# Attention without a partner pass: four heads at once, and the output list cut into halves of the queries

## The chip, the cores and the metric

The kernel runs on one core of one Trainium2 chip. The metric is the device time of one execution in microseconds, as the median of several runs. Engines are named as in the profile: PE is TensorE (matmuls; PEld its weight loads), DVE is VectorE, ACT is ScalarE, POOL is GpSimd, and SP is the queue from which the DMAs of this kernel are issued. A profile comes from one profiled execution. "Granted clock" is the share of TensorE's full clock that the throttle let through.

## What is computed

Six sublayers act on an input of 8 sequences, 1024 tokens and 256 features, all in float32: a mixture of experts, causal attention, the same mixture of experts again, then a channel mix, a state-space layer and the channel mix again. The change touches only the attention, and the front of the second mixture of experts, which is run from the attention's work lists. Cut to these:

```python
def _L0_attn_ref(x, w_qkv, w_out, b_out):        # x: 8 x 1024 x 256, 16 heads of 16
    qkv = jnp.einsum('btd,de->bte', x, w_qkv).reshape(B, T, 3, h, Hd)
    ...
    logits = jnp.einsum('bhqd,bhkd->bhqk', q, k) * scale
    logits = logits + (1.0 - mask)[None, None, :, :] * big_neg      # causal
    attn = jax.nn.softmax(logits, axis=-1)
    out = jnp.einsum('bhqk,bhkd->bhqd', attn, v)
    ...
    return jnp.einsum('btd,de->bte', out, w_out) + b_out

x = x + 0.5 * _L0_ffn_ref(_layernorm(x), ...)
x = x + _L0_attn_ref(_layernorm(x), L0_attn_w_qkv, L0_attn_w_out, L0_attn_b_out)
x = x + 0.5 * _L0_ffn_ref(_layernorm(x), ...)     # its front: logits = xf @ Wr + br, softmax
...
```

## The kernel before

**Passes and units.** The 16 heads of a sequence are worked on in 4 groups of 4 heads (`HG`), so there are 32 groups. Group t needs two things in turn: the maximum of each query's logits (queries on the partitions, `self.rows`), and then, with the maximum folded into the transposed queries, the exponentials (keys on the partitions, `self.cols`) and their products with the values. `Attention.run` pipelines the two: in pass t it takes the maxima of group t (`now`) and, beside them, the exponentials of group t - 1 (`old`). Passes are numbered from 0 to 32. Pass 0 has no `old` and pass 32 has no `now`: these are the two passes without a partner. Each pass has 12 units (u = 0 to 11); a unit is one tile of 128 rows with 128 to 512 columns for each of the 4 heads. The widths of units 0 to 11 in `old` are 512, 384, 256, 128, then five times 512, then 384, 256, 128; in `now` they are 512, 384, 256, 128, four times 512, and 512, 384, 256, 128.

**Inside a unit.** A unit is written in two parts. Part 0 issues the logits (L724) of heads 0 and 1 for `now` and of heads 2 and 3 for `old`; part 1 has them the other way round. A head fills 32 rows of the array, so the four heads of a part lie in different row groups and can run side by side. The results go to PSUM: `s1`, 3 banks, for `now`, and `s2`, 3 banks, for `old`. VectorE takes the maxima from s1 (L737, L740), ScalarE the exponentials from s2 into `pT` (L767), GpSimd cuts the diagonal block (L773). The products with the values (`sums`, L787) of a unit follow in part 0 some units later (`LAG`), collect in one bank `po`, and are copied to `so` (L793) and stored to the DRAM tensor `kept` (L796) once for each half of 512 queries: at the end of unit 3's columns for queries 0 to 511, and at the end of unit 11's for 512 to 1023. `less_max` (L749 to L758) sends the negated maxima through DRAM into rows of the transposed queries, in unit 4 of a pass for the first half and in unit 0 of the next for the second.

**Work lists.** Everything else is cut into steps and dealt out between the units by `Lists`. A list is a generator that yields `""` (a step that has no matmul) or `"pe"` (one that has). In each part one `""` step is taken, and in part 1 of each unit but 0 and 4 also one `"pe"` step; the first list whose next step is of the wanted kind gives it. `drain` runs all remaining steps of a list at once. The lists are:

- `steps_in`: layer norm, transposes, queries and keys (pq, L692), values (pv, L655) of the next sequence; added in front in unit 2 of a sequence's third pass, drained at the end of the fourth. `steps_qk` (four pq) is the second half of queries and keys; added in front in unit 2 of a sequence's first pass.
- `steps_out`: division by the sum of the exponentials and projection. It loads the sums from `kept` (over_p, L809) and the unnormalised output (oT, L811), takes the reciprocal (L816), sends it through DRAM (over_d, L819; over, L821), spreads it over the partitions with a matmul (pr, L828) and multiplies oT by it (L833), four times; then four projections (pp, L841), each added to `xt` (L847). There are eleven `""` steps ahead of the first pr. At its end it goes on with `store` and `steps_front`, the front of the second mixture of experts: layer norm, four transposes (tr, L673, copied by ScalarE, L871), four router matmuls (pl, L880; bias added by VectorE, L884), softmax (L890 to L900) and a store.

All matmuls of the lists share one PSUM bank (`mm`). `bank` first flushes the `Pipe`, which issues what reads the bank before, so the next matmul of a list waits for that reader. The list `outs` of sequence b is added in unit 3 of the first pass in which `old` belongs to sequence b + 1 (pass 4b + 5), has four passes, and is drained where the next one is added. The one of the last sequence runs alone after the loop. Each engine works through its instructions in the order in which they are issued.

Of the kernel before, what the change touches and what calls it, by code (L numbers as in the profile page):

```python
# [8 lines left out]
F32 = mybir.dt.float32  # L9
# [3 lines left out]
ALU = mybir.AluOpType  # L13
# [4 lines left out]
P = 128  # L18
D = 256
KC = D // P  # L20
# [10 lines left out]
H = 16  # L31
HD = 16
HS = 32
HG = P // HS
NG = H // HG
# [461 lines left out]
class Attention:  # L497
# [5 lines left out]
    W = 512  # L503
# [211 lines left out]
                to, self.padded[name, p % 2][i].rearrange("h s t -> (h s) t")  # L715
            )

    def logits(self, name, out_of, heads):

        got = {}  # L720
        for h in heads:
            lhsT, rhs = out_of(slice(h * HS, (h + 1) * HS))
            s = self.pools[name].tile([P, self.W], F32, name=name)
            self.net.nc.tensor.matmul(s[:, 0 : rhs.shape[-1]], lhsT, rhs, start=True, stop=True)  # L724
            got[h] = s
        return got
# [70 lines left out]
                q.kept[g * HG : (g + 1) * HG, :, a : a + W].rearrange("h s t -> (h s) t"), so  # L797
            )

    def steps_out(self, q, store):  # L800


        net, nc = self.net, self.net.nc
        T, W = net.T, self.W
        yield ""
        n = H // KC
        q.oT = self.pools["oT"].tile([P, KC, T], F32, name="oT")
        sp = self.pools["over"].tile([P, H * T // P], F32, name="over_p")
        nc.sync.dma_start(sp, q.kept[:, HD, :].rearrange("h (i t) -> h i t", t=H * T // P))  # L809
        for k in range(KC):  # L810
            nc.sync.dma_start(q.oT[:, k, :], q.kept[k * n : (k + 1) * n, 0:HD, :])  # L811
        for _ in range(3):
            yield ""

        yield ""
        nc.vector.reciprocal(sp, sp)  # L816
        yield ""
        d = self.pools["dram"].tile([H, T], F32, name="over_d")
        nc.sync.dma_start(d.rearrange("h (i t) -> (h i) t", t=H * T // P), sp)  # L819
        q.over = self.pools["over"].tile([H, T], F32, name="over")  # L820
        nc.sync.dma_start(q.over, d)  # L821
        for _ in range(5):
            yield ""
        for t0 in range(0, T, W):
            for k in range(KC):
                yield "pe"
                pr = self.bank([P, W], "pr")
                nc.tensor.matmul(  # L828
                    pr, self.spread[:, k, :], q.over[:, t0 : t0 + W], start=True, stop=True
                )  # L830

                def take(o=q.oT[:, k, t0 : t0 + W], pr=pr):
                    nc.vector.tensor_tensor(o, pr, o, ALU.mult)  # L833

                self.pipe.filled(take)
        for c0 in range(0, net.NT, 2):
            yield "pe"
            po = self.bank([P, 2, D], "pp")
            for c in range(2):
                for k in range(KC):  # L840
                    nc.tensor.matmul(  # L841
                        po[:, c, :], q.oT[:, k, (c0 + c) * P : (c0 + c + 1) * P],
                        self.wo[:, k, :], start=(k == 0), stop=(k == KC - 1),
                    )

            def take(x=q.x[:, c0 : c0 + 2, :], po=po):
                nc.vector.tensor_tensor(x, x, po, ALU.add)  # L847

            self.pipe.filled(take)
        yield ""  # L850
        self.pipe.flush()
        yield from store(q.x, q.b)

    def steps_front(self, moe, x, b, rows, S):
# [61 lines left out]
    class Lists:  # L916
# [28 lines left out]
    def run(self, pools, load, store):  # L945
        net = self.net
        self.pools, self.pipe, work = pools, self.Pipe(), self.Lists()
        net.nc.scalar.preload_act_table_set("natural_log_exp_and_others")
        seqs = [self.Sequence(b) for b in range(net.B)]
        groups = [(q, g) for q in seqs for g in range(NG)]  # L950
        LAG, U = 2, len(self.rows)
        ins = work.add(self.steps_in(seqs[0], lambda x: load(x, 0)))
        work.drain(ins)
        behind = []
        outs = ins

        for t in range(len(groups) + 1):
            now = groups[t] if t < len(groups) else None
            old = groups[t - 1] if t else None
            if now:  # L960
                q, g = now
                nxt = seqs[q.b + 1] if q.b + 1 < net.B else None
                qT, kT = self.q[t % 3], self.k[t % 3]
            if old:
                oqT, okT = self.q[(t - 1) % 3], self.k[(t - 1) % 3]
            for u in range(U):
                if now:
                    i, k0, k1 = self.rows[u]
                if old:
                    a, j = self.cols[u]  # L970
                    q0 = max(a, j * P)
                    pT = pools["pT"].tile([P, HG, self.W], F32, name="pT")
                for part, (ha, hb) in enumerate((((0, 1), (2, 3)), ((2, 3), (0, 1)))):
                    if now:
                        sa = self.logits(
                            "s1", lambda r: (qT[r, i * P : (i + 1) * P], kT[r, k0:k1]), ha
                        )
                    if old:
                        sb = self.logits(
                            "s2", lambda r: (okT[r, j * P : (j + 1) * P], oqT[r, q0 : a + self.W]),  # L980
                            hb,
                        )
                    self.pipe.flush()
                    if now:
                        self.maxima(self.rows[u], t, sa)
                    if old:
                        self.weights(self.cols[u], sb, pT)
                    if part == 0:
                        while len(behind) > LAG - bool(old):
                            self.sums(*behind.pop(0))  # L990
                        work.take("")
                        continue
                    if old:
                        self.causal(self.cols[u], pT)
                        behind.append((self.cols[u], *old, pT))
                    if u == 0 and old:
                        self.less_max(t - 1, 1)
                    elif u == 4 and now:
                        self.less_max(t, 0)
                    else:  # L1000
                        work.take("pe")
                    work.take("")
                if u == 2 and now:
                    if g == 1:
                        work.drain(qk)
                    if g < NG - 1:
# [30 lines left out]
class Layer1:  # L1037
# [9 lines left out]
    W = 512  # L1047
# [855 lines left out]
```

## Time and profile before

| what | us |
|---|---|
| median of 3 runs | 5663.02 (5660.18 to 5664.28) |
| the profiled execution | 5670.78 |
| its span, first to last instruction | 5668.9 |
| mean granted clock of TensorE | 0.890 |

The median is of the plain runs; the profile's numbers belong to the one profiled execution, whose span is 0.1% above that median. Within it, from the trace's windows:

| stretch, us from the span's start | what runs | length | PE busy | DVE busy | ACT busy | clock |
|---|---|---|---|---|---|---|
| 705.4 to 754.1 | pass 0 (`now` alone) | 48.7 | 44.7 | 26.9 | 2.6 | 0.72 |
| 754.1 to 2169.7 | passes 1 to 31 | 1415.6 | 1398.6 | 961.0 | 827.2 | 0.99 |
| 2169.7 to 2230.8 | pass 32 (`old` alone) | 61.1 | 55.0 | 0.9 | 23.4 | 0.56 |
| 2230.8 to 2268.6 | out list of the last sequence | 37.8 | 17.9 | 6.5 | 1.3 | 0.62 |
| 2268.6 to 2294.6 | its front of the mixture of experts | 26.0 | 12.0 | 10.5 | 4.3 | 0.58 |

A pass with both partners lasts 1415.6 / 31 = 45.7 us. The rest of the span, before and behind, belongs to stages that the diff doesn't touch. In the lines of the profile that follow, a timeline row has the start, the length, the engine, the source line, the operation, the tile written and the tiles read, the number of equal records merged, and in brackets the idle time before it with what ended it; a float32 matmul leaves two records for each matmul issued. A row of the windows has the stretch, its length, each engine's busy time with its number of records, then the granted clock, the share of the DMA engines and GB/s. Ends of matmuls are modelled, so a busy PE isn't one at its peak.

### The profile page before, as it was taken

To read this page: it belongs to the slowest core of one execution; us is meant where nothing else is said; L and a number is where in the kernel's file an instruction comes from. 1 tells how busy PE (TensorE), PEld (TensorE's weight loads), DVE (VectorE), ACT (ScalarE), POOL (GpSimd) and SP (SyncE) were. 2 spreads that over 40 slices of the span, in tenths; PEclk is the share of its full clock that TensorE was granted. 3 is DMA by queue.
4 is the path that set the end of the run, shared out by engine and by line. 5 is a ranking of instruction groups with operands and counts; after the bars stand their busy time and mean duration, and the time that the engine had idled before them with its cause. 6 is when DMAs were issued, how large, how long until landed. Compare 5 with 4: busy or idle time off the path is not lost.

```text
span 5668.9 us, 60303 instructions
## 1 busy us (share of the span) xinstructions
PE 4660.3 (82%) x21302; PEld 2227.0 (39%) x21302; DVE 3431.4 (61%) x5653; ACT 2505.6 (44%) x4152; POOL 2205.0 (39%) x1801
## 2 busy tenths in 40 slices
PE   5599699999999998399776778788787778878867
PEld 5355434444444443255532233333333324333324
DVE  4532166667666762633107877777767777677884
ACT  2011145666565553011144645465464645546443
POOL 1244201111111110234316656556555666556662
PEclk7699889999999997599887889889898888989888
DMA  6123312122221220223206454535536463454652
GB/s 201 33 57 60 79 37 75 58 74 68 81 74 59 77 69 27 68 49 62 44 13 156 134 145 122 153 98 143 138 105 158 110 163 108 112 153 114 169 137 63
DMA packets 252976, 545.28 MB, mean 96 GB/s; under 512 B 29681, under 2 KB 143681, under 8 KB 252674
## 3 DMA queue, kind: packets, MB, share of 16 engines
q1 hardware_dynamic: 228098, 507.34, 32.1%
q0 software_dynamic: 24576, 34.10, 3.7%
q8 instruction: 168, 2.75, 0.2%
q14 instruction: 134, 1.10, 0.1%
HBM read 400.31 MB, written 141.03 MB: 95 GB/s over the span
## 4 chain that ended last, share of the span: by engine, by line
PE 25%; DVE 13%; ACT 6%; issue 5%; DMA 2%; POOL 1%; SPq 0%; DVEq 0%; POOLq 0%; ACTq 0%
DVE h L1719 8%; PE y L1647 5%; PE pc L1366 4%; PE pr L1261 4%; PE pk L1239 4%; PE pu L1417 2%; DVE hc L1724 2%; PE pp L1501 2%; ACT h L1625 2%; PE pd L1432 1%; ACT xn L1195 1%; PE px L1396 1%; DMA sdu<-du 1%; DVE ln_st L1182 1%; ACT L1131 1%
## 5 line engine op out<-in xcount | busy, mean ns | idle before, releaser
L767 ACT ACTIVATE pT<-s 128x512 f32<-128x512 f32 (+3 forms) x1536 | 670.7, 488 | 554.9 <-PE s L724 546.7
L1625 ACT ACTIVATE h<-sdl,A 128x1024 f32<-128x1024 f32 x512 | 567.0, 1112 | 644.4 <-DVE hc L1724 622.4
L724 PE MATMUL s<-kT,qT 32*128 32x512 f32 (+3 forms) x3072 | 839.5, 540 | 12.9 <-DVE mx L740 8.0
L1647 PE MATMUL y<-hc,pick 128*32 128x512 f32 x2048 | 648.5, 714 | 227.6 <-DVE hc L1724 227.6
L724 PE MATMUL s<-qT,kT 32*128 32x512 f32 (+3 forms) x3072 | 763.7, 547 | 13.3 <-ACT pT L767 13.3
L1616 POOL TENSOR_TENSOR dbu<-sdu,b 128x1024 f32<-128x1024 f32 x256 | 602.3, 2353 | 405.3 <-DMA sdu<-du 217.5
L1719 DVE TENSOR_TENSOR_SCAN h<-h,dbu 128x1024 f32<-128x1024 f32 x256 | 586.1, 2289 | 184.4 <-ACT h L1625 159.8
L1719 DVE TENSOR_TENSOR_SCAN h<-h,sdu 128x1024 f32<-128x1024 f32 x256 | 586.2, 2290 | 160.6 <-ACT h L1625 146.3
L1724 DVE TENSOR_TENSOR hc<-h,c 128x1024 f32<-128x1024 f32 x512 | 625.6, 1222 | 30.4 <-PE y L1647 2.5
L773 POOL TENSOR_SCALAR_AFFINE_SELECT pT<-pT 128x512 f32<-128x512 f32 x256 | 162.4, 634 | 1180.7 <-ACT pT L767 1097.2
L1616 POOL TENSOR_TENSOR sdu<-sdu,b 128x1024 f32<-128x1024 f32 x256 | 602.4, 2353 | 14.4 <-DMA b<-bc 3.7
L724 PEld LDWEIGHTS s<-kT,qT 32*128 32x128 f32 x3072 | 327.6, 187 | 437.1 <-DVE mx L740 184.6
L466 ACT ACTIVATE mid<-pm,bu 128x512 f32<-128x512 f32 x192 | 131.6, 686 | 734.3 <-PE pm L462 734.3
L737 DVE TENSOR_REDUCE part<-s 128x1 f32<-128x512 f32 x512 | 329.7, 685 | 187.1 <-PE s L724 186.5
L487 POOL DMA_INDIRECT acc<-o,idx x128 | 211.2, 1650 | 502.0 <-DVE o L484 229.7
L1647 PEld LDWEIGHTS y<-hc,pick 128*32 128x32 f32 x2048 | 126.7, 125 | 712.0 <-issue 391.4
L740 DVE CUSTOM_DVE_ANT_0 junk<-s,mask,part 128x256 f32<-128x256 f32 (+3 forms) x512 | 281.5, 550 | 159.7 <-PE s L724 114.7
L462 PE MATMUL pm<-tT,wu 128*128 128x512 f32 x768 | 364.0, 612 | 0.0
L479 PE MATMUL po<-wd,mid 128*128 128x256 f32 x1536 | 352.0, 393 | 0.0
L787 PE MATMUL po<-pT,at_v 128*32 128x512 f32 (+3 forms) x3072 | 337.1, 512 | 0.3 <-POOL pT L773 0.3
L740 DVE CUSTOM_DVE_ANT_0 junk<-s,mask 128x256 f32<-128x256 f32 (+3 forms) x512 | 250.4, 489 | 136.5 <-PE s L724 84.9
L479 PEld LDWEIGHTS po<-wd,mid 128*128 128x128 f32 x1536 | 305.1, 200 | 44.3 <-issue 1.0
(262 smaller groups left out, 6736.8 us busy)
## 6 DMA issues: line engine op xcount, KB each, us to landing
sdl<-dl SPq DMA_DIRECT2D x256, 512.0 KB
sdu<-du SPq DMA_DIRECT2D x256, 512.0 KB
acc<-xt SPq DMA_DIRECT2D x24, 1024.0 KB
xt<-acc SPq DMA_DIRECT2D x24, 1024.0 KB
rows<-moe_r SPq DMA_DIRECT2D x16, 1056.0 KB
qT<-padded_q SPq DMA_DIRECT2D x32, 512.0 KB
kT<-padded_k SPq DMA_DIRECT2D x32, 512.0 KB
kept<-so SPq DMA_DIRECT2D x64, 256.0 KB
```

Source lines behind the costliest of these rows:

```text
L462: nc.tensor.matmul(pm, wu[:, k, n * P : (n + 1) * P], tT[:, k, t0 : t0 + HALF], start=(k == 0), stop=(k == KC - 1),)
L479: nc.tensor.matmul(po, mid[:, n, j * P : (j + 1) * P], wd[:, n, :], start=(n == 0), stop=(n == NF - 1),)
L724: self.net.nc.tensor.matmul(s[:, 0 : rhs.shape[-1]], lhsT, rhs, start=True, stop=True)
L737: nc.vector.tensor_reduce(part, sh, AX.X, ALU.max)
L740: nc.vector.tensor_tensor_reduce(junk[:, 0:w], sh[:, 0:w], self.mask[:, W - w : W], 1.0, part if a else -3e38, ALU.add, ALU.max, self.mx[n ...
L767: self.net.nc.scalar.activation(pT[:, h, 0:w], sh[:, 0:w], AF.Exp, scale=1.0 / HD**0.5)
L787: nc.tensor.matmul(q.po[h * HS : (h + 1) * HS, o:W], self.va[q.b % 2][:, j, g * HG + h, :], pT[:, h, 0 : W - o], start=(j == 0), stop=(j = ...
L1616: nc.gpsimd.tensor_tensor(inputs[i], t, seqs[b].rep["b", p], ALU.mult)
L1625: nc.scalar.activation(decays[i], spread["dl", i - p], AF.Exp, scale=self.A[:, p, n : n + 1])
L1647: nc.tensor.matmul(self.py[g * self.RG : (g + 1) * self.RG, t0 : t0 + W], self.pick[:, j, :], hc[:, t0 : t0 + W], start=False, stop=(j == ...
L1719: nc.vector.tensor_tensor_scan(decays[i], decays[i], inputs.pop(i), 0.0, ALU.mult, ALU.add)
L1724: nc.vector.tensor_tensor(hc, decays.pop(i), seqs[b].rep["c", p], ALU.mult)
```

## The change

- In a pass without a partner, part 0 takes all four heads and part 1 none. Two of the four go to banks of `s1` and two to banks of `s2`, so the pass uses all six. In pass 32, one more `"pe"` step may be taken in part 0.
- `steps_out` works on one half of the queries (512), from column `a`: loads, reciprocal, round trip through DRAM, two pr and two pp. `steps_end` is the second half followed by `store` and the front.
- The first half's list (`half`) is added in unit 8 of the pass in which `old` is the last group of a sequence (pass 4b + 4); there `outs` of the sequence before is drained first. The second half's list is added in unit 3 of the next pass, where `outs` was added before; there `half` is drained first. After the last pass, `half` is drained and the second half follows.

```diff
-    def logits(self, name, out_of, heads):
+    def logits(self, names, out_of, heads):
         got = {}
-        for h in heads:
+        for name, h in zip(names, heads):
...
-    def steps_out(self, q, store):
+    def steps_out(self, q, a):
...
-        q.oT = self.pools["oT"].tile([P, KC, T], F32, name="oT")
-        sp = self.pools["over"].tile([P, H * T // P], F32, name="over_p")
-        nc.sync.dma_start(sp, q.kept[:, HD, :].rearrange("h (i t) -> h i t", t=H * T // P))
+        q.oT = self.pools["oT"].tile([P, KC, W], F32, name="oT")
+        sp = self.pools["over"].tile([P, H * W // P], F32, name="over_p")
+        nc.sync.dma_start(
+            sp, q.kept[:, HD, a : a + W].rearrange("h (i t) -> h i t", t=H * W // P)
+        )
         for k in range(KC):
-            nc.sync.dma_start(q.oT[:, k, :], q.kept[k * n : (k + 1) * n, 0:HD, :])
+            nc.sync.dma_start(q.oT[:, k, :], q.kept[k * n : (k + 1) * n, 0:HD, a : a + W])
...
-        for t0 in range(0, T, W):
-            for k in range(KC):
+        for k in range(KC):
...
-        for c0 in range(0, net.NT, 2):
+        for c0 in range(0, W // P, 2):
...
+    def steps_end(self, q, store):
+        yield from self.steps_out(q, self.W)
         yield from store(q.x, q.b)
...
                 for part, (ha, hb) in enumerate((((0, 1), (2, 3)), ((2, 3), (0, 1)))):
+                    na, nb = ("s1", "s1", "s2", "s2"), ("s2", "s2", "s1", "s1")
+                    if not (now and old):
+                        ha = hb = range(HG) if part == 0 else ()
+                    sa, sb = {}, {}
...
                     if part == 0:
                         while len(behind) > LAG - bool(old):
                             self.sums(*behind.pop(0))
+                        if not now:
+                            work.take("pe")
                         work.take("")
                         continue
...
                 if u == 3 and old and old[1] == 0 and old[0].b:
+                    work.drain(half)
+                    outs = work.add(self.steps_end(seqs[old[0].b - 1], store))
+                if u == 8 and old and old[1] == NG - 1:
                     work.drain(outs)
-                    outs = work.add(self.steps_out(seqs[old[0].b - 1], store))
+                    half = work.add(self.steps_out(old[0], 0))
...
         while behind:
             self.sums(*behind.pop(0))
-        work.drain(outs)
-        self.pipe.flush()
-        outs = work.add(self.steps_out(seqs[-1], store))
+        work.drain(half)
+        outs = work.add(self.steps_end(seqs[-1], store))
         work.drain(outs)
         self.pipe.flush()
```

More of the change, by code (lines that the diff above doesn't have):

```diff
@@ L798, in sums @@
             )
-    def steps_out(self, q, store):
+    def steps_out(self, q, a):
         net, nc = self.net, self.net.nc
-        T, W = net.T, self.W
+        W = self.W
         yield ""
         n = H // KC
-        q.oT = self.pools["oT"].tile([P, KC, T], F32, name="oT")
-        sp = self.pools["over"].tile([P, H * T // P], F32, name="over_p")
-        nc.sync.dma_start(sp, q.kept[:, HD, :].rearrange("h (i t) -> h i t", t=H * T // P))
+        q.oT = self.pools["oT"].tile([P, KC, W], F32, name="oT")
[3 more added lines that the diff above has]
+        )
         for k in range(KC):
-            nc.sync.dma_start(q.oT[:, k, :], q.kept[k * n : (k + 1) * n, 0:HD, :])
+            nc.sync.dma_start(q.oT[:, k, :], q.kept[k * n : (k + 1) * n, 0:HD, a : a + W])
         for _ in range(3):
@@ L817, in steps_out, with take @@
         yield ""
[L818 to L821, printed above, removed]
+        d = self.pools["dram"].tile([H, W], F32, name="over_d")
+        nc.sync.dma_start(d.rearrange("h (i t) -> (h i) t", t=H * W // P), sp)
+        over = self.pools["over"].tile([H, W], F32, name="over")
+        nc.sync.dma_start(over, d)
         for _ in range(5):
             yield ""
-        for t0 in range(0, T, W):
-            for k in range(KC):
[L826 to L835, printed above, removed]
-        for c0 in range(0, net.NT, 2):
+        for k in range(KC):
+            yield "pe"
+            pr = self.bank([P, W], "pr")
+            nc.tensor.matmul(pr, self.spread[:, k, :], over, start=True, stop=True)
+            def take(o=q.oT[:, k, :], pr=pr):
+                nc.vector.tensor_tensor(o, pr, o, ALU.mult)
+            self.pipe.filled(take)
+        for c0 in range(0, W // P, 2):
             yield "pe"
@@ L844, in steps_out, with take @@
                     )
-            def take(x=q.x[:, c0 : c0 + 2, :], po=po):
+            def take(x=q.x[:, a // P + c0 : a // P + c0 + 2, :], po=po):
                 nc.vector.tensor_tensor(x, x, po, ALU.add)
@@ L973, in run @@
                 for part, (ha, hb) in enumerate((((0, 1), (2, 3)), ((2, 3), (0, 1)))):
+                    na, nb = ("s1", "s1", "s2", "s2"), ("s2", "s2", "s1", "s1")
+                    if not (now and old):
+                        ha = hb = range(HG) if part == 0 else ()
+                    sa, sb = {}, {}
                     if now:
                         sa = self.logits(
-                            "s1", lambda r: (qT[r, i * P : (i + 1) * P], kT[r, k0:k1]), ha
+                            na, lambda r: (qT[r, i * P : (i + 1) * P], kT[r, k0:k1]), ha
                         )
@@ L979, in run @@
                         sb = self.logits(
-                            "s2", lambda r: (okT[r, j * P : (j + 1) * P], oqT[r, q0 : a + self.W]),
+                            nb, lambda r: (okT[r, j * P : (j + 1) * P], oqT[r, q0 : a + self.W]),
                             hb,
```

## The prediction

> **What bounds the kernel now.** I read the page first (82% TensorE busy, but an average over four stages), then the windows of the attention stage, which the change is confined to, then the timeline inside three of them. All times are in the profiled execution.
>
> ```profile
> core 0: us, PE busy (x) PEld busy (x) DVE busy (x) ACT busy (x) POOL busy (x), PEclk, DMA share, GB/s
> 747.10:774.40 27.30, 27.21 (x113) 14.27 (x117) 14.87 (x58) 6.58 (x18) 2.54 (x4) 0.50 0.13 47
> 774.40:777.80 3.40, 3.40 (x18) 1.01 (x11) 0.97 (x3) 1.41 (x4) 0.00 (x0) 0.50 0.00 0
> 1074.00:1120.00 46.00, 46.00 (x344) 19.14 (x342) 30.21 (x91) 26.81 (x62) 5.07 (x8) 1.00 0.20 59
> 2173.90:2177.30 3.40, 2.90 (x23) 1.43 (x26) 0.00 (x0) 3.05 (x9) 0.95 (x2) 1.00 0.02 4
> 2177.30:2180.70 3.40, 2.93 (x15) 0.62 (x8) 0.00 (x0) 0.87 (x3) 0.32 (x1) 0.50 0.20 78
> 2186.00:2216.00 30.00, 26.79 (x80) 6.13 (x80) 0.00 (x0) 11.34 (x21) 0.55 (x1) 0.50 0.02 9
> ```
>
> Passes 1 to 31 (row 1074:1120) are TensorE-bound at full clock with VectorE close behind; any TensorE time lost there is lost. The last pass (row 2186:2216) runs at half clock with ScalarE 38% busy: it is a chain, not a full engine:
>
> ```profile
> 2197.03 1.93 PE L787 MATMUL po<-pT,at_v 128*32 128x512 f32 x8
> 2198.89 2.08 PE L724 MATMUL s<-qT,kT 32*128 32x512 f32 x6
> 2201.00 1.57 ACT L767 ACTIVATE pT<-s 128x512 f32<-128x512 f32 x3 [3.27 <-PE s L724]
> 2201.65 2.07 PE L724 MATMUL s<-qT,kT 32*128 32x512 f32 x2 [0.67 <-ACT pT L767]
> 2203.65 1.93 PE L787 MATMUL po<-pT,at_v 128*32 128x512 f32 x8
> ```
>
> One unit takes 6.62 us (2197.03 to 2203.65). Three heads (x6, two records a head) run side by side in 2.08 us; the fourth finds its three banks taken and costs another 2.07. After the last pass the out list of the last sequence stands alone, and then its front:
>
> ```profile
> 2236.20 0.32 SPq L819 DMA_DIRECT2D over_d<-over_p  x1
> 2242.52 0.32 SPq L821 DMA_DIRECT2D over<-over_d  x1
> 2244.54 2.07 PE L828 MATMUL pr<-over,spread 16*128 16x512 f32 x2 [14.39 <-DMA over<-over_d]
> 2284.06 1.88 PE L880 MATMUL pl<-wr,moe_xT 128*128 128x8 f32 x8 [0.67 <-ACT moe_xT L871]
> 2285.97 0.17 DVE L884 TENSOR_TENSOR moe_lg<-pl,br 128x16 f32<-128x16 f32 x1 [5.72 <-PE pl L880]
> 2286.20 1.88 PE L880 MATMUL pl<-wr,moe_xT 128*128 128x8 f32 x8 [0.27 <-DVE moe_lg L884]
> ```
>
> The last three lines matter most: lists drained at once go through one bank, matmul, VectorE, matmul. The same steps in pass 8, spread one to a unit, never wait:
>
> ```profile
> 1109.87 0.66 PE L673 MATMUL tr<-ident,moe_r 128*128 128x128 f32 x4
> 1113.47 1.06 PE L880 MATMUL pl<-wr,moe_xT 128*128 128x8 f32 x8
> 1116.75 1.06 PE L880 MATMUL pl<-wr,moe_xT 128*128 128x8 f32 x8
> ```
>
> **The clock.** It changes only at steps of 3.41 us. I weighted each matmul record by the share of the array's rows and columns it fills and by its columns at 0.495 us for 512 (a pq step: four records in 1.98 us; a 512-column logit record is then 0.495 x 1/4), and summed over these steps for the attention stage. The five steps before a fall hold 0.00 to 0.33 of a step, the 41 that stay at half at most 0.41, the five before a rise 0.42 to 0.56, the 421 that stay full at least 0.42. So what counts is work in the array, with a line near 0.42, not occupancy: at 2173.9 TensorE was 85% busy by records and fell, and from 747 to 774 it was full at half clock for 27 us without rising.
>
> **Gains.** *Pass 0* (48.7 us). The four heads of a unit go out together, so a unit with a pq step loses one bank wait. VectorE's pitch (0.84, 0.70, 0.58, 0.45 us a head by width, 0.65 for a reduction, 0.90 to 0.51 with the old maximum) sums to 32 us, so the gain is between 0 and 16.7. Walking it: four pq steps stay between units, at half clock (3.7 us) or full (2.0); units 4 to 7 each save about 1.2 to 2. I take 7.
>
> *Last pass* (2170.9, first exponential, to 2230.2, last copy of so: 59.3 us). Cold: logits 6x2.08 + 2x1.65 + 2x1.22 + 2x0.80 = 19.8, sums 6x1.93 + 2x1.51 + 2x1.08 + 2x0.65 = 18.1, 12 gaps of 0.1, the end 1.5: 41, a gain of 18. Warm: ScalarE sets it, 24x0.545 + 8x0.435 + 8x0.33 + 8x0.225 = 21.0, plus copy, max and gaps of some 4.5, plus 1.5: 27, a gain of 32. A wide unit then holds 1.98 us of array work in 2.3 us (0.86, the narrow ones 0.5 or more), above 0.42, so I expect it warm. I take 28.
>
> *Out list of the last sequence* (2230.2 to 2268.6: 38.4 us). The first half's loads, reciprocal and round trip go out in units 9 to 11; its four bank rounds (2 x 2.86 cold, then pp, about 11 us) run while the second half's rows land, but the second reciprocal stands behind them on VectorE. Then 0.5 + about 4 for the round trip (6.3 before, behind 1 MB of oT loads, now landed) and half of the 24.1 us of rounds, with the first pp cold: 12.9. 29 us in all, gain 9.5 (7 to 12). Gains: 44.5 (25 to 60).
>
> **Losses.** The instruction order of the changed program shows what is moved. *Unit 8 of passes 8, 12 ... 28* (six times): draining outs there issues all four pl steps of the front and its softmax in one go; before they took units 9, 10, 11 and unit 1 of the next pass. In the walk of pass 8: tr ends at 1110.5, its copy stands behind two exponentials on ScalarE and ends at 1111.6; four rounds of 1.06 + 0.27 end at 1116.8; lg, max, subtract, exponential, sum, reciprocal, products and copy (about 1.8 us) hold VectorE, which starts unit 9 at 1118.6 and not 1111.77: 6.8 late. Behind the waiting pl stand unit 9's logits, behind the softmax unit 9's maxima. In return units 9 to 1 become VectorE-bound: 13.9 us (four heads at their pitch) for the 16.4 they took. Net 4.3. But these 6.5 us hold nearly no array work (eight columns a matmul), so a whole step lies under 0.33 and the clock falls: two rounds at 2.14, and unit 9 at half clock. There its 2.48 us of array work in 5.3 give 0.47, so it rises after one or two steps: net 7. If it only rises with the pp steps of unit 3, as pass 1 did after 27 us: 13. I take 7.5: 45 us (26 to 78).
>
> *Unit 3 of passes 5, 9 ... 29* (seven times): the half list is added at unit 8, needs eleven free steps before its first pr (unit 2), and is drained at unit 3: pr, pp, pp in a row. pp waits for the product (VectorE backlog, 0.69), the second for the sum: 6.8 us for 5.0 of matmuls. Elsewhere pr moves from units 9 to 1 to 2 and 3, two pp from units 2 to 6, where they cost 2.0 each, to 11 and 1, where VectorE's bound hides 0.4 to 0.7. Net 2 to 3, and a fall of the clock at some phases, 0.7: 3 each, 21 us (7 to 28).
>
> *Halved DMAs and reciprocals.* Ten DMAs for five in a list, 3.4 us of SP time a sequence: SP waits for over_d to land (1.5 us), and minus_max behind it is wanted only four units later; cover gone, 1.5 us a time, 11 in all. The 0.94 us reciprocal becomes two; the one in unit 11 stands where VectorE bounds: 0.5 to 0.9, seven times, 4. Losses: 70 (33 to 117).
>
> **A rule that speaks differently.** The Trainium skill, TensorE: Matmul & The Clock Gate, Why this matters for your kernels, says the clock is kept if TensorE has no idle gap over about 3 us between bursts. In the drain no gap exceeds 1.2 us; by it the clock would hold and the losses be 6x4.3 + 7x2.3 + 4 = 46, about no change overall. The fall at 2177.3, with gaps under 1 us, is against it.
>
> **Sum.** 70 - 44.5 = +25 us on the median 5663.0 (the profiled execution, 5670.8, and its span, 5668.9, are 0.1% above it; the difference carries over): 5688.
>
> **Rivals.** *Cheap drains* (ends faster): the clock holds or comes back inside the drain. Losses 26 + 7 + 0 to 3, gains 48: about 5650. For it: the pp rounds alone keep it full (2259 to 2268, 73% busy). Against: pl fills eight columns. It decides if a drain at unit 8 costs less than 4 us. *Cold carry-over* (slower): the clock stays half to the next pass's unit 3; 13 each, 78 + 28 + 4 less 44: 5729. For it: pass 1. Against: pass 1 had no sums in units 0 and 1. *The last pass doesn't warm up*: gain 18, 5698; so the part that ought to pay does half. *They cancel*: 5652 to 5674.
>
> **How the numbers follow.** Drains outweigh, warm last pass 0.38; cold carry-over 0.12; last pass cold 0.10; cancel 0.15; cheap drains 0.25. About 0.2% (11 us) is what a measurement of this kernel can tell from no change: faster 0.25, same 0.15, slower 0.60. The likeliest case by itself spans 5675 to 5712; to leave out two in ten, 5640 to 5736.
>
> **What would show it.** After unit 8 of pass 8 four pl rounds with DVE moe_lg as releaser and a granted clock of 0.5 behind them; pp waiting for DVE oT in unit 3; passes of a period of four averaging 2.5 us more; the last pass in 27 us at clock 1.0; 29 us from the last copy of so to the last sum into xt. I am wrong if the clock stays 1.0 through the drains, or if VectorE, not TensorE, had slack enough to take them.

## The result and the profile after

The changed kernel took 5710.32 us in the median of 4 runs (5704.2 to 5717.54), beside 5661.60 us for the kernel before in the same comparison: a ratio of 1.0082, with a 95% interval of 1.0066 to 1.0098. It is 49 us slower; the prediction said 25 slower.

The two profiled executions differ by less than that: the span after is 5702.5 us, that before 5668.9, so 33.6 us. The difference is in a part that the change doesn't touch. The first logits of the attention start 690.6 us after the span's start now and started at 705.4 before, 14.8 us of nothing that the change did. So the stage is compared from its own first logits to the store at the end of its last front: 1588.8 us before, 1638.8 after, 50.0 us more, which agrees with the medians. All that follows is counted inside this stage.

First the windows of the changed kernel: pass 0, passes 1 to 31, pass 32, the last out list, its front. They are cut as the table of before was, but for one edge: the fourth row begins where the last copy of so starts (2275.1), and before it began where that copy ends. The columns are the stretch, its length, each engine's busy time with its records, then the granted clock.

```profile
690.60:729.40 38.80, 34.18 (x115) 12.47 (x115) 25.68 (x74) 2.61 (x5) 0.00 (x0) 0.74 0.14 46
729.40:2248.70 1519.30, 1457.13 (x10150) 622.60 (x10149) 961.25 (x2901) 829.41 (x1868) 209.45 (x359) 0.96 0.20 63
2248.70:2275.10 26.40, 25.74 (x218) 8.88 (x215) 1.39 (x7) 20.99 (x53) 5.74 (x9) 1.00 0.13 45
2275.10:2304.00 28.90, 18.96 (x40) 10.01 (x39) 5.95 (x10) 1.87 (x2) 0.52 (x2) 0.70 0.09 31
2304.00:2329.40 25.40, 11.98 (x48) 9.95 (x48) 10.36 (x45) 4.30 (x8) 1.57 (x9) 0.55 0.46 128
```

Every end of the stage is shorter: 38.8 us for 48.7, 26.4 for some 61 (now at clock 1.00), and the last out list 28.9 for 38.4, both from the start of the last copy of so. The middle, where the new lists are dealt out and drained, is 1519.3 for 1415.6, while VectorE and ScalarE are busy for just as long as before (961 and 829 us). So VectorE and ScalarE have no more work; what grew is waiting, and TensorE's time at half clock (0.96 for 0.99).

A table by kind of pass shows where. Passes with the same remainder by 4 do the same steps; each number is the sum over the passes of its row, in us, from the trace, a pass being counted from the transposition of the maxima (pm) in its unit 0 to the next one, and pass 0 from the first logits. The two right-hand columns belong to experiments told below.

| what | before | after | change | e11, no drains, late store | e4, halves for the last sequence alone |
|---|---|---|---|---|---|
| passes 0 and 1 | 99.4 | 85.8 | -13.6 | 86.7 | 86.4 |
| 8, 12 ... 28 (drain in unit 8) | 276.5 | 330.7 | +54.2 | 279.2 | 276.9 |
| 5, 9 ... 29 (drain in unit 3) | 281.5 | 330.4 | +48.9 | 301.3 | 283.3 |
| 6, 10 ... 30 | 325.7 | 318.0 | -7.7 | 309.2 | 325.4 |
| 7, 11 ... 27 | 308.8 | 322.1 | +13.3 | 324.0 | 312.5 |
| 2, 3, 4, 31 | 175.7 | 173.3 | -2.4 | 174.0 | 174.6 |
| last pass, to the start of the last copy of so | 57.1 | 24.1 | -33.0 | 24.1 | 24.1 |
| last out list | 38.4 | 28.9 | -9.5 | 27.5 | 28.3 |
| its front | 25.6 | 25.4 | -0.2 | 25.1 | 25.4 |
| the stage | 1588.8 | 1638.8 | +50.0 | 1551.0 | 1536.9 |

Gains of 58.7 (13.6 + 2.4 + 33.0 + 9.5 + 0.2) stand against losses of 108.7 (54.2 + 48.9 - 7.7 + 13.3).

Now the drain in unit 8 of pass 8, in the timeline of the changed kernel:

```profile
1090.15 1.06 PE L882 MATMUL pl<-wr,moe_xT 128*128 128x8 f32 x8 [1.13 <-ACT moe_xT L873]
1091.24 0.17 DVE L886 TENSOR_TENSOR moe_lg<-pl,br 128x16 f32<-128x16 f32 x1 [1.13 <-PE pl L882]
1091.47 1.88 PE L882 MATMUL pl<-wr,moe_xT 128*128 128x8 f32 x8 [0.27 <-DVE moe_lg L886]
1093.62 1.87 PE L882 MATMUL pl<-wr,moe_xT 128*128 128x8 f32 x8 [0.27 <-DVE moe_lg L886]
1095.76 1.87 PE L882 MATMUL pl<-wr,moe_xT 128*128 128x8 f32 x8 [0.27 <-DVE moe_lg L886]
1097.56 1.01 PE L724 MATMUL s<-kT,qT 32*128 32x384 f32 x2
```

This is the picture that the prediction drew: four rounds with VectorE's bias addition (moe_lg) as releaser, the first 1.06 us long, the next three 1.87, which is half clock. Nothing of the next unit runs before 1097.56. The windows, cut near the clock's own steps, show the fall; the clock is the third number from the end:

```profile
1087.90:1091.30 3.40, 2.18 (x20) 1.39 (x12) 1.72 (x7) 1.56 (x3) 0.64 (x1) 1.00 0.45 124
1091.30:1094.70 3.40, 2.96 (x13) 2.87 (x14) 0.29 (x2) 0.00 (x0) 0.00 (x0) 0.50 0.03 10
1094.70:1098.10 3.40, 3.13 (x16) 2.99 (x20) 0.57 (x3) 0.00 (x0) 0.00 (x0) 0.50 0.00 0
```

TensorE is busy in 2.96 and 3.13 of 3.40 us and runs at half clock all the same. The clock falls at 1091.31 and is back at 1101.55, three of its steps of 3.41 us later, when the logits and sums of unit 9 have filled one.

The drain in unit 3 of pass 9, in the timeline:

```profile
1119.37 1.02 PE L829 MATMUL pr<-over,spread 16*128 16x512 f32 x2
1121.17 1.99 PE L840 MATMUL pp<-wo,oT 128*128 128x256 f32 x8 [0.78 <-DVE oT L832]
1123.21 0.69 DVE L846 TENSOR_TENSOR xt<-xt,pp 128x512 f32<-128x512 f32 x1 [2.09 <-PE pp L840]
1123.95 1.99 PE L840 MATMUL pp<-wo,oT 128*128 128x256 f32 x8 [0.78 <-DVE xt L846]
1125.87 0.70 PE L724 MATMUL s<-kT,qT 32*128 32x512 f32 x2
```

pr, VectorE's product, pp, VectorE's sum, pp: the next logits start 6.5 us after pr. The pp rounds fill the array (1.99 us for eight records is full clock) and the clock stays.

Last, the two ends that pay, in the timeline: wide units of pass 32, and in the last out list the first pr of the second half.

```profile
2262.21 2.17 ACT L767 ACTIVATE pT<-s 128x512 f32<-128x512 f32 x4
2263.54 1.52 PE L724 MATMUL s<-qT,kT 32*128 32x512 f32 x8
2264.76 2.06 ACT L767 ACTIVATE pT<-s 128x512 f32<-128x512 f32 x4 [0.38 <-PE s L724]
...
2289.41 2.04 PE L829 MATMUL pr<-over,spread 16*128 16x512 f32 x2 [4.54 <-DMA over<-over_d]
```

Four heads' logits (x8) go out in 1.52 us where three and then one took 4.2, ScalarE follows with four exponentials in 2.1 to 2.2, and a wide unit takes some 2.5 us in place of 6.62. In the out list TensorE waits 4.54 us for the second reciprocal's round trip, where the whole list waited 14.39.

### The profile page after: what moved, and what is told of

Same layout as the page of the kernel before. It is cut to its first block, busy times and chain, and to the rows that moved or that the text cites. A ratio compares the mean times of both kernels' runs of the same rounds, so it can differ in the third digit from the quotient of the medians.

```text
span 5702.5 us, 60380 instructions
## 1 busy us (share of the span) xinstructions
PE 4669.6 (82%) x21302; PEld 2229.7 (39%) x21302; DVE 3430.4 (60%) x5661; ACT 2506.8 (44%) x4152; POOL 2204.0 (39%) x1801
## 4 chain that ended last, share of the span: by engine, by line
PE 26%; DVE 12%; ACT 6%; issue 5%; DMA 2%; POOL 1%; SPq 0%; DVEq 0%; POOLq 0%; ACTq 0%
DVE h L1730 8%; PE y L1658 5%; PE pc L1377 4%; PE pr L1272 4%; PE pk L1250 4%; PE pu L1428 2%; DVE hc L1735 2%; PE pp L1512 2%; ACT h L1636 2%; DMA sdu<-du 1%; PE pd L1443 1%; PE po L479 1%; ACT xn L1206 1%; PE px L1407 1%; PE pm L462 1%
## 5 line engine op out<-in xcount | busy, mean ns | idle before, releaser
L724 PE MATMUL s<-kT,qT 32*128 32x512 f32 (+3 forms) x3072 | 851.8, 544 | 27.5 <-DVE mx L740 15.9
L724 PE MATMUL s<-qT,kT 32*128 32x512 f32 (+3 forms) x3072 | 758.3, 545 | 16.6 <-ACT pT L767 16.6
```

## Experiments

Times of different comparisons are set beside one another by their ratios to the kernel before, which was run with each; "by kind of pass" means the sums of the table above, from each run's own trace.

**1. The passes alone and the lists alone.** e1 is the kernel before with the part of the diff in `run` that gives four heads to part 0 in passes 0 and 32; e2 is the changed kernel without that part, so (against the changed kernel):

```diff
-                    na, nb = ("s1", "s1", "s2", "s2"), ("s2", "s2", "s1", "s1")
-                    if not (now and old):
-                        ha = hb = range(HG) if part == 0 else ()
+                    na, nb = ("s1", "s1"), ("s2", "s2")
...
-                        if not now:
-                            work.take("pe")
```

> The kernel before with one part of the change alone: passes 0 and 32 take four heads at a time in all six banks; the out lists stay whole and stand where they stood. If the gains of the changed kernel's ends come from the passes alone, passes 0 and 1 give back 13.6 us and the last pass 33 us, as in the changed kernel: about 5661 - 47 = 5615 (5608 to 5622), the last out list unchanged at 38.4 us. If the warm last pass was owed to the first half's loads and rounds moved into it, the clock falls in it again and the gain is 10 to 20: 5641 to 5651.

> The changed kernel's two lists for the halves, with passes 0 and 32 as before (two heads to a part, own banks). If the loss is the lists' alone, passes 1 to 31 lengthen by about 106 us as in the changed kernel and the last out list shortens by 9.5: about 5661 + 96 = 5757 (5745 to 5768). If the loss came from how the four-headed passes leave the clock or the banks (the cold carry-over of the prediction's rival), 5700 or less.

Measured: e1 5615.25 us, ratio 0.9915 (0.990 to 0.993); e2 5758.21 us, ratio 1.0158 (1.0143 to 1.0173). Both are where the additive reading put them. In e1 passes 0 and 1 take 86.0 us and the last pass 24.1, at clock 1.0 with no list beside it; in e2 the last pass is back at 58.1 us with the halves' loads in it, and the last out list is at 29.6. So the warm last pass is owed to the four heads alone, the shorter end to the halves alone, and the loss in the middle to the lists alone: nothing was carried over from one to the other.

**2. Halves for the last sequence only.** e4 has the four-headed passes, the whole out list of before for sequences 0 to 6, and the two halves for sequence 7, so (against e1):

```diff
+                if u == 8 and not now:
+                    work.drain(outs)
+                    half = work.add(self.steps_half(seqs[-1], 0))
...
-        outs = work.add(self.steps_out(seqs[-1], store))
+        work.drain(half)
+        outs = work.add(self.steps_end(seqs[-1], store))
```

> Four heads at a time in passes 0 and 32, whole out lists for the first seven sequences, and two halves for the last sequence alone. The sum of the parts that gained in the changed kernel: 13.6 at passes 0 and 1, 33 in the last pass, 9.5 in the last out list: 5661 - 56 = 5605 (5598 to 5612). If the gain of the last out list depends on half lists in every sequence, 5615.

Measured: 5606.15 us, ratio 0.9896 (0.9881 to 0.991). All three gains add up, and the kernel beats the one before and the changed one. Its median is the lowest of this study.

**3. What makes the clock fall in the drain.** e5 leaves the drain in unit 8 and puts work in: two dense matmuls ahead of each pl round.

```diff
-            pl = self.bank([P, 2, E], "pl")
+            pl = self.bank([P, 2, 256], "pl")
+            if self.warm:
+                for _ in range(2):
+                    nc.tensor.matmul(pl, xT[:, 0, 0:P], xT[:, 1, 0:512], start=True, stop=True)
```

> The changed kernel, with two more matmuls (128 rows and columns, 512 wide, their result overwritten) ahead of each of the four pl rounds of the drain in unit 8, six times: more work, put in to keep the array busy. By the prediction's theory of the clock (work in the array, weighted by rows and columns, a line near 0.42 of a step) a round of 1.98 + 1.06 + 0.27 us holds 0.6 of a step and the clock stays 1.0: unit 8 takes 12.9 + 8 - 3.5 = 17.4 and unit 9 loses its 0.9, +3.6 to +5 us a time, +22 to +30 in all on the changed kernel's 5710: about 5736. If the clock falls for another reason (TensorE waiting on VectorE between short rounds, or the gaps as such), the rounds run at half speed, 4 x (3.96 + 1.87 + 0.27) = 24.4 in place of 8.6: +95, about 5805.

Measured: 5737.90 us, ratio 1.0141 (1.0121 to 1.0161). The timeline of e5 in pass 8, and two windows, of the step in which its drain begins and of the next:

```profile
1104.53 1.98 PE L882 MATMUL pl<-moe_xT 128*128 128x512 f32 x4 [0.27 <-DVE moe_lg L889]
1106.36 0.95 PE L885 MATMUL pl<-wr,moe_xT 128*128 128x8 f32 x8
1107.58 1.98 PE L882 MATMUL pl<-moe_xT 128*128 128x512 f32 x4 [0.27 <-DVE moe_lg L889]
```

```profile
1099.30:1102.70 3.40, 2.27 (x15) 1.10 (x8) 1.61 (x6) 1.56 (x3) 0.64 (x1) 1.00 0.44 124
1102.70:1106.10 3.40, 3.13 (x14) 1.90 (x13) 0.17 (x1) 0.00 (x0) 0.00 (x0) 1.00 0.02 7
```

The gaps are the same 0.27 us, TensorE is busy for the same 3.13 of 3.40 us as in the last of the drain's windows above, and the clock is 1.00 in place of 0.50, in all six drains. Unit 8 takes 16.6 us (17.4 expected). The step ahead is alike too: TensorE was busy in 2.18 us of it in the changed kernel and in 2.27 in e5, behind which the clock fell in the one and held in the other. What e5 adds is work in the array, so at equal occupancy by records it is this work that parts the two.

**4. Each drain taken away by itself.** e7 moves `drain(outs)` from unit 8 to unit 3; e8 leaves out `drain(half)` in unit 3. In e8, and in e3 below, the first half's projection reads the second half's rows, as the list kept its oT with the sequence. e7:

```diff
                 if u == 3 and old and old[1] == 0 and old[0].b:
+                    work.drain(outs)
                     work.drain(half)
...
-                    work.drain(outs)
                     half = work.add(self.steps_out(old[0], 0))
```

and e8:

```diff
-                    work.drain(half)
                     outs = work.add(self.steps_end(seqs[old[0].b - 1], store))
```

> The changed kernel without the drain in unit 8: the pl steps are dealt out over units 9, 10, 11 and 1 as before, and the first half's list stands behind them, so that the drain in unit 3, which stays, issues one pr more. If the drain in unit 8 costs the 9 us a time that the passes show, 6 x 9.2 = 55 less, given back 6 x 0.5 to 2 in unit 3: 5658 to 5668. By the prediction's 7.5 a time: 5668 to 5677. If a step that isn't drained costs as much elsewhere, near 5700.

> The changed kernel without the drain in unit 3: the second list is added there behind the first, whose two pp steps then go out one by one in units 5 and 6; the table loads of passes 7, 11 ... move to unit 1. If the drain in unit 3 costs the 5.5 us a time that the passes show, 7 x 5.5 = 38 less: about 5672 (5665 to 5679); by the prediction's 3 a time 5689. If the pp steps cost as much in units 5 and 6, where the kernel before had pp steps, 5700 or more.

Measured: e7 5701.41 us, ratio 1.0082 (1.0058 to 1.0105); e8 5714.65 us, ratio 1.0095 (1.0078 to 1.0113). Neither saved anything that can be told from the changed kernel's 1.0082: the saving that each expectation put first failed to come, by 33 to 50 us, and the times are those of the last case of each. By kind of pass each drain did give back about what was expected, and the passes behind it took it:

- e7: passes 8 ... 28 fall to 277.2, as before the change (-53.5). But passes 5 ... 29 rise from 330.4 to 357.3, since the drain in unit 3 has one round more in six of the seven, and passes 6 ... 30 from 318.0 to 327.4.
- e8: passes 5 ... 29 fall from 330.4 to 297.6 (-32.8). But passes 6 ... 30 rise from 318.0 to 355.7. That is not the dealt-out steps alone: VectorE waits 30.1 us there, in six waits, for the load that experiment 5 is about.

The timeline of e7 in pass 9 shows the first of these:

```profile
1128.73 1.02 PE L829 MATMUL pr<-over,spread 16*128 16x512 f32 x2
1130.53 2.07 PE L829 MATMUL pr<-over,spread 16*128 16x512 f32 x2 [0.78 <-DVE oT L832]
1133.39 3.55 PE L840 MATMUL pp<-wo,oT 128*128 128x256 f32 x8 [0.78 <-DVE oT L832]
```

A pr round fills 16 of 128 rows. In the six drains that have two of them in a row the clock falls within 4 us of the first, here at 1129.7, behind a step that holds 0.43 of work as the prediction weighs it; the second pr and the first pp run at half speed. The fourth round cost 27 us in six drains, 4.5 us each; pass 5, which has none, took 47.3 us as in the changed kernel.

**5. Both drains taken away.** e3 leaves both out, each list behind the unfinished ones; e10 is the same with each list's own oT.

> The changed kernel without the two drains inside the loop: half is added in unit 8 and the second list in unit 3 as there, each list behind the ones that are not finished, and the steps are dealt out one by one. If the drains are the loss, it keeps all gains (56 us below the kernel before) and pays 0 to 13 us for the doubled DMAs, reciprocals and the moved table loads: 5605 to 5620. If halving the list is itself the cost (ten DMAs for five, two reciprocals, steps moved beside VectorE's work), it stays near 5700.

> The changed kernel without both drains, as in the earlier run of that kind, but each list keeps its own oT, so that the first half's projection reads the first half's rows. The order of the instructions is that of the earlier run, so the same 5662 (5655 to 5668) if the rows that it read wrongly had nothing to do with its time; 5605 to 5620 if they had.

Measured: e3 5662.32 us, ratio 1.0000 (0.9988 to 1.0012); e10 5664.56 us, ratio 1.0005 (0.9994 to 1.0016). The first expectation of e3, 5605 to 5620, fell; e10 shows that the rows read had nothing to do with it. Without a drain inside the loop half lists still ate the whole gain. By kind of pass the largest part of the excess sits in 6, 10 ... 30: 355.3 us in e10, 325.7 before (17 us more stand in 5, 9 ... 29 and 11 in 7, 11 ... 27). The rows of the statistics of the next sequence (L600) say why; this is e10, whole stage:

```profile
L600 DVE BATCH_NORM_STATS2 ln_st<-xt x96: 407/414/429, 987.8 to 1987.2; 128x6 f32<-128x256 f32 x96
its engine sat idle before it (us, times) until:
  DMA xt<-acc: 29.9, 6
```

VectorE stood still for 5.0 us, six times, until the load of the next sequence had landed. The kernel before has no such wait. In the changed kernel it is there too, 9.1 us in six; SP's queue and VectorE in its pass 10:

```profile
1163.34 0.69 DVE L846 TENSOR_TENSOR xt<-xt,pp 128x512 f32<-128x512 f32 x1 [0.84 <-PE pp L840]
1164.05 0.38 SPq L1835 DMA_DIRECT2D acc<-xt  x1
...
1166.32 1.17 SPq L1832 DMA_DIRECT2D xt<-acc  x1
1176.53 0.75 DVE L600 BATCH_NORM_STATS2 ln_st<-xt 128x6 f32<-128x256 f32 x2 [2.13 <-DMA xt<-acc]
```

The halves end in unit 1 of pass 10, so the store of the finished sequence (L1835) now stands on SP just ahead of the next group's rows and the next sequence's load. It waits for the last sum into xt (1163.34), and everything behind it waits too: the load goes out at 1166.32, 4.67 us after the store of so (kept, 1161.65), and shares the DMA engines with the 1 MB of the store: from 6 to 9 us behind the load's issue they are still 82% busy (22% in e9, below). In e10 the load goes out 8.88 us after the store of so in this pass.

**6. The store moved.** e9 is the changed kernel with that store behind the front; e11 is e10 with the same.

```diff
             def store(xt, b):
-                nc.sync.dma_start(of(acc[1], b), xt)
                 yield from at.steps_front(moe, xt, b, rows[1], S)
+                nc.sync.dma_start(of(acc[1], b), xt)
```

> The changed kernel with the store of a finished sequence (acc from xt, 1 MB) issued behind its front in place of ahead of it; no other instruction is moved. In passes 6, 10 ... 30 of the changed kernel that store stands on SP waiting for the last sum into xt, the load of the next sequence stands behind it, and VectorE's statistics wait 2.1 us for that load. If that queueing (and the store's traffic beside the load) is the wait, the load goes out some 2 to 3 us sooner, the wait goes, and with it the clock's falls in these passes: they come to about 42.5 to 43.5 from 45.4, 7 x 2 to 2.9 = 14 to 20 less: 5690 to 5696. If the statistics only come up too early for a load of this size, the wait stays: 5705 to 5712.

> The same kernel without both drains, with the store of a finished sequence issued behind its front. In the earlier run without drains the statistics of the next sequence waited 4.7 us for the load that stood behind this store, the clock fell, and passes 6, 10 ... 26 took 51 us, 4.6 more than before the change. If the store in the queue is the cause, these passes come down to 43 to 45: 6 x 6 to 8 = 36 to 48 less than without this step, 5614 to 5626, and half lists without drains and without that wait cost at most 20 us above the kernel with halves for the last sequence alone (5606). If it isn't, 5655 or more.

Measured: e9 5705.35 us, ratio 1.0078 (1.0059 to 1.0096); e11 5613.90 us, ratio 0.9905 (0.9886 to 0.9924). In e9 the queue runs on (the load 1.40 us after the store of so), and the statistics wait for nothing:

```profile
1173.28 0.39 SPq L796 DMA_DIRECT2D kept<-so  x1
...
1174.68 0.43 SPq L1832 DMA_DIRECT2D xt<-acc  x1
...
1185.95 0.74 DVE L600 BATCH_NORM_STATS2 ln_st<-xt 128x6 f32<-128x256 f32 x2
```

Passes 6 ... 30 come down from 318.0 to 307.1, 11 us where 14 to 20 were expected (six of the seven to 43.2 or 43.3, as expected; pass 30, which loads no sequence, stays at 47.7), and the median by 5 (2 by the ratios), which the intervals can't tell from nothing: in e9 the mechanism is shown by the trace, its price by the trace only. In e11 it is plain: these passes fall from 355.3 to 309.2, 46 us, the stage of the profiled execution by 39 and the median by 51. So the early store, not the halving, took most of the gain of the kernel without drains; beside e4 its stage is still 14 us longer (1551.0 and 1536.9). The move takes away the store's place in the queue and its traffic beside the load together, and no run parts these two.

With the store out of the way in both, e9 and e11 differ by the two drains alone. The one in unit 8 costs 331.4 - 279.2 = 52 us, 8.7 a time; the one in unit 3 costs (331.5 + 307.1) - (301.3 + 309.2) = 28 us, 4.0 a time. For unit 8 there is a second pair: e8 and e3 differ by that drain alone, and passes 8 ... 28 take 326.7 and 276.5 us there, 8.4 a time, with no difference in passes 5 ... 29 (297.6 and 297.8).

**7. The table loads of passes 7, 11 ... 27.** These passes lengthened by 13.3 us, and none of their steps is drained. What changed in them is that ScalarE's logarithm and exponential for the front's layer norm, which load a table each, came from unit 2 to unit 0. The timeline of the changed kernel in pass 7:

```profile
1003.78 1.28 ACT L609 ACT_TABLE_LOAD   x1
1005.07 0.21 ACT L609 ACTIVATE ln_r<-ln_v 128x8 f32<-128x8 f32 x1
1005.30 1.28 ACT L610 ACT_TABLE_LOAD   x1
1006.59 0.21 ACT L610 ACTIVATE ln_r<-ln_r 128x8 f32<-128x8 f32 x1
1007.38 0.58 PE L724 MATMUL s<-qT,kT 32*128 32x384 f32 x1 [1.57 <-ACT pT L767]
```

TensorE waits 1.57 us for exponentials that stand behind the two loads. e6 puts four empty steps ahead of the store and the front:

```diff
         yield from self.steps_out(q, self.W)
+        for _ in range(4):
+            yield ""
         yield from store(q.x, q.b)
```

> The changed kernel with four empty steps ahead of the front's layer norm, which puts ScalarE's logarithm and its two table loads back into unit 2 of passes 7, 11 ... 27, where the kernel before had them; nothing else moves. If the 13 us by which these passes lengthened come from the table loads standing in unit 0, where TensorE waits for the exponentials and the clock falls, about 5710 - 13 = 5697 (5692 to 5702). If they come from something else in these passes, no change.

Measured: 5686.69 us, ratio 1.0048 (1.0031 to 1.0065), 24 us under the changed kernel's median and 19 by the ratios, more than the 13 expected, and for another reason. Passes 7 ... 27 gave back 2.6 us only (322.1 to 319.5). Passes 6 ... 30 gave back 19.2 (318.0 to 298.8): the empty steps also moved the store behind the load and the statistics of the finished sequence out of pass 10, so that "nothing else moves" was wrong. In part it is experiment 6 by other means; the moved statistics are in its 19.2 too.

What the lengthening of passes 7 ... 27 does follow in the changed kernel is the clock. The one pass in which it held took 51.6 us, as before (51.5), with unit 0 longer by 1.9 us and units 1 and 2 shorter by 1.9 together; those with one step of 3.4 us at half clock took 53.1 and 53.2; those with two took 54.7, three times. That the moved table loads thin a step's work out until the clock falls is argued, not shown. In e6, with the loads back in unit 2, it still fell in two of six, and the passes in which it held took 52.5. In e10 the loads stand in unit 1, the clock held in five of six, and these took 52.8, so that the six took 319.9 all the same. And in e4, where these passes have the lists and loads of before, it fell in two of six (53.3 us each). What makes these passes longer stays open.

## Why the prediction came out as it did

- **The direction, and the reason for it**, were right: lists drained at once through one bank outweigh what the ends gain. The "cold carry-over" (the clock stays low to the next pass's unit 3) did not happen: it came back two or three of its steps after it fell, in unit 9, as the likeliest case had it. "Cheap drains" fell with the 8.7 us that e9 and e11 show for unit 8 (it needed less than 4), "the last pass doesn't warm up" with the clock of 1.00 there, "they cancel" with the median of 5710.32. Of the signs named, the passes of a period of four are longer by 4.2 us on average (108.7 over 26 passes), not 2.5. One reading was loose: in the row that was to show VectorE "close behind" TensorE, it is busy 66% of the time.
- **Gains** were put at 44.5 and were 58.7. The last out list is exact, 9.5 predicted and 9.5 measured, but with some luck: the second half's first pr starts 14.3 us behind the start of the last copy of so (15.5 reckoned), and from there to the last sum it is 14.6 (12.9 reckoned). The last pass was mis-sized at 28: 33.0, five more. ScalarE sets its pace as reckoned (21.0 us of exponentials expected, 20.99 us busy in all), but little stands around it. Pass 0 was put at 7: it gave 9.9, and pass 1 another 3.7, which the prediction hadn't counted: the clock of pass 1 is 0.89 in place of 0.79.
- **The drain in unit 8** was put at 7.5 a time, 45 in all: 54.2 by the table, 52 by e9 against e11, 50 by e8 against e3. The walk of its rounds is right to a tenth (1.06, then some 2.14 a round), but for three rounds at half clock where two were reckoned; the return was put too high. By ScalarE's first exponential of each unit, unit 8 is 8.9 us longer, unit 9 takes 0.8 more for its half clock, and units 10 and 11 give back 0.3 to 0.4 each and unit 1 of the next pass 0.5.
- **The drain in unit 3** was put at 3 a time, 21 in all. By itself it costs 4.0, 28 in all, the upper end of its range. The drain was reckoned about right: 6.5 us from its pr to the next logits, 6.8 in the prediction. So was a pp in units 11 and 1, 2.0 less the 0.4 to 0.7 that VectorE's bound hides: these two units are longer by 1.3 each. The mis-sized term is what a pp costs in units 2 to 6, put at 2.0: in e9, where the statistics wait for nothing, units 2, 3, 5 and 6 of passes 10, 14 ... have lost one each and are shorter by 1.0 to 1.4 only.
- **Two terms are missing.** "Ten DMAs for five" looked at SP's own time and at minus_max behind it, and put them at nothing with a bound of 11; the DMA that got in the way was one that the diff doesn't touch, the store of the sequence, which moved up in SP's order because the list ends sooner: 11 us by e9. And passes 7 ... 27: 13 us, whose cause stays open (experiment 7). The prediction followed the matmuls of the moved lists, and of the steps without a matmul only the DMAs and the reciprocals of the halves themselves.

In sum, from the predicted 25: 14 more gained, 9 and 7 more lost in the two drains, 11 by the store in SP's queue and 13 in passes 7 ... 27 make 51, beside 50.0 measured. The reciprocals' 4 can't be told apart.

The theory of the clock held better than its use. Summed as in the prediction (each record by its share of rows and columns and by its columns), 17 of the 18 steps before a fall in the changed kernel's attention hold 0.00 to 0.35 of a step and one 0.43; the 414 that stay full hold at least 0.43; the 17 before a rise 0.44 to 0.56. One line near 0.43 parts them but for the one fall that stands on it, and e5 is the experiment on it.

The Trainium skill, TensorE: Matmul & The Clock Gate, Why this matters for your kernels, keeps the clock if no gap between bursts exceeds about 3 us; here it fell in all six drains of unit 8 though the longest gap in the one shown is 1.13 us. The same page, A second HAM failure mode: psum-queue depth-cycling, lets it fall by many short idles between groups of matmuls; e5 kept every one of these idles (0.27 us) and the clock held. By these measurements it is the work in the array that counts.

## What to carry to other kernels

A list that is drained in one go costs a round trip per bank (matmul, reader, matmul) for each step that is left, so count the steps left at the drain, and whether they fill the array. A shorter list brings everything behind it forward, loads and stores and table loads included: follow each of those in its own queue, not only the matmuls. Here that was shown for a store and a load (e10, e11). And cut a change into its parts first: here the parts that touch the ends alone make the kernel 1.0% faster (e4), and the whole made it 0.8% slower.

## What the runs showed of the hardware that wasn't expected

- A DMA that waits on SP holds back those behind it: the store waiting for xt moved a load by some 3 us (4.67 less 1.40; 8.88 less 1.42 in e10 beside e11), and the load's consumer then waited 2.1 us (5.0 on average in e10).
- Half clock comes with TensorE 87 and 92% busy by its records (2.96 and 3.13 of 3.40 us): the matmuls in them, of 8 columns each, hardly count. Two dense matmuls a round kept the clock at 1.00.
- Two table loads with their two activations take 3.02 us on ScalarE (1003.78 to 1006.80), 1.5 us for each switch. The Trainium skill, ScalarE: Activation LUTs, What ACT_TABLE_LOAD costs, has the same load (about 1283 ns) and adds some 1380 ns of drain to each switch; no such drain shows in this trace, where the activation follows 0.01 us after the load's end.
